# Freeing a PSUM bank with a ScalarE copy, and issuing GpSimd's DMAs from SyncE, in a perceiver layer

## The chip, the cores and the metric

One NeuronCore of a Trainium2 chip runs the whole layer in one launch. The metric is device time in microseconds (us). The engines are TensorE (PE: matmuls; its weight loads are listed apart as PEld), VectorE (DVE), ScalarE (ACT), GpSimd (POOL) and SyncE (SP, which here only issues DMAs). Each engine works through its own instructions in order and waits on semaphores. PSUM, where matmul results arrive, is used here as eight banks of 128 partitions x 512 fp32.

## The reference

Three residual blocks in fp32 on x of 4 x 256 x 256: cross-attention of x on a context of 4 x 4096 x 256, causal linear attention with exponential features, and a gated feed-forward block. Nearly all the time, and all of the change, lies in the first.

```python
def _L0_xattn_ref(query, key, value, Wq, bq, Wk, bk, Wv, bv, Wh, bh):
    Q = query @ Wq.T + bq
    K = key @ Wk.T + bk
    V = value @ Wv.T + bv
    ...
    dot = jnp.einsum('bhsd,bhtd->bhst', Q, K) / np.sqrt(D_HEAD)
    scores = jax.nn.softmax(dot, axis=-1)
    out = jnp.einsum('bhst,bhtd->bhsd', scores, V)
    out = out.reshape(B, T_src, D_MODEL)
    return out @ Wh.T + bh
...
x = x + _L0_xattn_ref(_layernorm(x, axis=-1), ctx_1024, ctx_1024, ...)
x = x + _L0_attn_ref(_layernorm(x, axis=-1), ...)
x = x + _L0_ffn_ref(_layernorm(x, axis=-1), ...)
```

There are 16 heads of 16 dimensions, 256 queries and 4096 context rows for each of 4 batches.

## The kernel before

**Units and steps.** The work is cut into 16 units `u`: a batch and four heads. A unit has 16 steps, one for each 256 context rows, so the main loop runs n = 0 to 256, with w = n modulo 16 the step within the unit. PE, ACT, DVE and SP execute in the order in which the program writes their instructions; the order on POOL is chosen by the framework.

**Softmax in two passes.** The exponentials need each query's maximum first. `maxima(s, heads)` makes it, 19 steps ahead (s = n + 19): for 128 of the queries and 512 context rows, one `pm` tile (a full PSUM bank, L843, two products) for each of four heads, which a `tensor_reduce` on DVE brings down to one column of `mx` (L849). Each step has four `pm` tiles, for heads 0 to 3. At w = 13, `shift(u + 1)` takes the maximum over all columns for the next unit (L857), splits it into a high and a low half `nhl`, and sends it with eight small DMAs as rows into `sh` (L869).

**A step.** `scores` makes for each head a tile `pt` of 256 context rows x 256 queries: a product of ones and `sh` brings the negative maxima in (L893), then four products of keys and queries (L902); `exps` takes the exponential on ACT into `e` (L910). `product` multiplies the previous step's `e` by the values into `pav` (L924), and `add` sums that on DVE into `av` (L938).

**Context items.** Keys and values of later units are made in the same loop. An item is a chunk of 512 context rows for eight heads (two units). Eight key items, then eight value items, are made over two units, each item in two halves, one a step. A half makes a tile `pc` (L183); its `out` brings `pc` to SBUF on ACT: `ku` for keys (L772), `v` for values (L805). For keys, POOL then splits `ku` into two halves `khl` (L752, L753), and SP sends these in four DMAs into the key tiles `kt` (L780). Key items fall into steps w = 8 to 15 of an even unit and w = 0 to 7 of the odd one after it. The item's context comes into one of four slots of `wff` (4 x 1024 of its 4608 columns; later `wff` takes the feed-forward weights). `load_context` issues one such load on SP (L737). Three are issued at the start, and one more when each item is constructed, that is just before its first half.

**Banks.** All PSUM tiles rotate through eight banks in the order in which the program allocates them: a new tile waits until the one allocated eight places before it has been read. In the steps that make maxima and an item's half, that order is pm2, pm3, pt0, pt1, pt2, pt3, pm0, pm1, pc, pav. So pc takes the bank of pm2, pav that of pm3, and in the next step the first six tiles take the banks of pt0 to pt3, pm0, pm1, and the last two `pm` those of pc and pav.

**The end of a unit.** At w = 0, `finish(u - 1)` writes `av` to DRAM (`scr`, L951, and the sums, L953) and, when `scr` has landed, reads it back in another layout (eight DMAs `oT`, L960, and two `dn`, L964), all on POOL; only for the last two units on SP. At w = 8, 9, 10 and 12 of the next unit its reciprocals (L970), its division (L974) and, for odd units, a projection (L987) follow.

**The end of the loop.** In the last steps the second block begins. `plan` lists its pieces by step, 0 being n = 240; the pieces at -4 are the loads of the feed-forward weights into `wff` (L432), which wait for the contexts there to be read. `att0` is a tile for this block's result that takes the place of an earlier one. After n = 236 no maxima are made any more, after n = 235 no items.

Of the kernel before, what the change touches and what calls it, by code (L numbers as in the profile page):

```python
# [12 lines left out]
F32 = mybir.dt.float32  # L13
# [3 lines left out]
ALU = mybir.AluOpType  # L17
AX = mybir.AxisListType
# [3 lines left out]
P = 128  # L22
# [18 lines left out]
def perceiver_layer(  # L41
# [406 lines left out]
    def start_causal():  # L448
# [43 lines left out]
        def call(f, *args):  # L492
            return lambda: f(*args)
# [16 lines left out]
            -15: [call(sq2, 0), v2], -14: [call(sq2, 1)],  # L510
            -13: [call(qk_normed, 0)], -12: [call(qk_normed, 1)],
            -11: [call(qk_turned, 0)], -10: [call(qk_turned, 1)],
            -4: [call(weight_load, n) for n in range(6)],
            -3: [call(features, 0)],
            -1: [steps[0][0]],
            0: [steps[0][1], steps[1][0]],
            1: [call(features, 2)],
# [162 lines left out]
def cross_attention(tc, xr, load_x, load_queries, load_rest, ctxT, wqP, bqu_sb, wkP, bk_sb, wvP, eps,  # L680
# [22 lines left out]
    with ExitStack() as st:  # L703
# [29 lines left out]
        def load_context():  # L733
            for i, (_, p, c) in itertools.islice(loads, 1):
                c0 = i % 4 * KC * CH
                t = wff[:, c0 : c0 + KC * CH].rearrange("p (k c) -> p k c", c=CH)
                nc.sync.dma_start(out=t, in_=ctxT[p // 2, c])  # L737
                contexts.append(t)

        def context(p, c):  # L740
            load_context()
            return contexts.pop(0)

        kts = {}
# [10 lines left out]
        def key(p, c, queues=(nc.sync,) * 4, engine=nc.gpsimd):  # L755

            m, x = p % 2, context(p, c)
            ku = upool.tile([P, CH], F32, tag="ku", name="ku", bufs=2)
            khl = upool.tile([P, 2, CH], F32R, tag="khl", name="khl", bufs=2)
            made = []  # L760

            def half(part, pk):
                made.append(pk)
                cs = slice(part * (CH // 2), (part + 1) * (CH // 2))
                for k in range(KC):
                    product4(
                        pk, wk_sb[:, k, m * P : (m + 1) * P], x[:, k, cs], start=k == 0, stop=k == KC - 1
                    )

            def out(part):  # L770
                cs = slice(part * (CH // 2), (part + 1) * (CH // 2))
                nc.scalar.activation(ku[:, cs], made.pop(), AF.Identity, bias=bk_sb[:, m : m + 1])  # L772
                if part == 0:
                    return
                halved((khl[:, 0], khl[:, 1]), ku, engine)
                for u in (2 * p, 2 * p + 1):
                    kts[u, c] = key_tile(u % 3, c, F32R)
                for h in range(4):
                    half, side = divmod(h, 2)
                    queues[h].dma_start(  # L780
                        out=kts[2 * p + half, c][side::2].bitcast(F32),
                        in_=khl[64 * half : 64 * half + 64, side].bitcast(F32),
                    )

            return half, out

        def value(p, c):

            m, x = p % 2, context(p, c)
            made = []  # L790

            def half(part, pv):
                pv = pv.rearrange("p (i t) -> p i t", t=P)
                made.append(pv)
                for i in range(2):
                    t0 = (2 * part + i) * P
                    for k in range(KC):
                        product4(
                            pv[:, i, :], x[:, k, t0 : t0 + P], wv_sb[:, k, m * P : (m + 1) * P],
                            start=k == 0, stop=k == KC - 1,  # L800
                        )

            def out(part):
                to = vs[:, c, 2 * part : 2 * part + 2, : 8 * (HD + 1)]
                nc.scalar.copy(  # L805
                    to.rearrange("p t (h d) -> p t h d", d=HD + 1)[:, :, :, :HD],
                    made.pop().rearrange("p t (h d) -> p t h d", d=HD),
                )

            return half, out  # L810

        def whole(item):
            half, out = item
            for part in range(2):
                half(part, bank([P, CH // 2], "pc"))
                out(part)
# [14 lines left out]
        def maxima(s, heads):  # L831

            u, w = divmod(s, NS)
            c, i = divmod(w, 2)
            if u not in mxs:
                mxs[u] = small.tile([P, 2, 4, NCH], F32, tag="mx", name="mx")
            mx, qa, kt = mxs[u], qas[u], kts[u, c]
            pms = [bank([P, CH], "pm") for _ in heads]

            def products(turn):  # L840
                for j, pm in zip(heads, pms):
                    rows = slice(32 * j, 32 * j + 32)
                    nc.tensor.matmul(  # L843
                        pm, lhsT=qa[rows, turn, i::2], rhs=kt[rows, :], start=turn == 0, stop=turn == 1
                    )

            def reduce():
                for j, pm in zip(heads, pms):
                    nc.vector.tensor_reduce(mx[:, i, j, c : c + 1], pm, AX.X, ALU.max)  # L849

            return products, reduce

        def shift(u):

            sh = shs[u] = small.tile([P, T], F32R, tag="sh", name="sh")
            neg = small.tile([P, 4, 2], F32, tag="neg", name="neg")
            nc.vector.tensor_reduce(neg.rearrange("p j i -> p i j"), mxs.pop(u), AX.X, ALU.max, negate=True)  # L857
            if u == 0:
                by_head = neg.rearrange("p j i -> p i j")
                hi, lo = neg0[:, :, :, 0], neg0[:, :, :, 1]  # L860
                nc.vector.tensor_copy(hi.bitcast(F32R), by_head)
                nc.vector.tensor_tensor(lo, by_head, hi, ALU.subtract)
            else:
                nhl = small.tile([P, 4, 2, 2], F32R, tag="nhl", name="nhl")
                halved((nhl[:, :, 0], nhl[:, :, 1]), neg, nc.vector)
                for j in range(4):
                    for side in range(2):
                        row = 32 * j + side
                        nc.gpsimd.dma_start(  # L869
                            out=sh[row : row + 1, :].rearrange("o (p i) -> o p i", i=2).bitcast(F32),  # L870
                            in_=nhl[:, j, side].bitcast(F32),
                        )

# [10 lines left out]
        def scores(n, heads):  # L884

            u, w = divmod(n, NS)
            kt, qa, sh = kts[u, w // 2], qas[u], shs[u]
            pts = [bank([P, 2, T], "pt") for _ in heads]

            def shifts():  # L890
                for j, pt in zip(heads, pts):
# [48 lines left out]
        def finish(u):  # L940
# [5 lines left out]

            b, q = divmod(u, NQ)
            av = avs.pop(u)
            queue = nc.sync if u >= NU - 2 else nc.gpsimd
            scr = dram.tile([P, T], F32, tag="scr", name="scr")  # L950
            queue.dma_start(out=scr, in_=av)  # L951
            sums = dram.tile([T // 16, 4, 16], F32, tag="sums", name="sums")
# [73 lines left out]
        with tc.manual_schedule(engines={ET.PE, ET.Activation, ET.DVE, ET.SP}):  # L1026
# [35 lines left out]
            qs[0][2](0, nc.vector)  # L1062
            normal[1][0]()
            unit_queries(0)
            whole(key(0, 0, (nc.sync, nc.scalar) * 2, nc.vector))
            unit_queries(1)
            for piece in normal[1][1:]:
# [47 lines left out]
            def all_maxima(g, between=None):  # L1115

                groups = [maxima(g, heads) for heads in ((0, 1), (2, 3))]
                for turn in range(2):
                    for products, _ in groups:
                        products(turn)  # L1120
                for _, reduce in groups:
# [18 lines left out]
            later = {}  # L1140
            plan = {}
            masks(wide.tile([P, 3, P], F32, tag="mask", name="mask"))
            att0 = wide.tile([P, KC, D], F32, tag="wk", name="att0")
            place["att"] = lambda b: att0
            tags = itertools.cycle(("ku", "khl"))
            place["at"] = lambda: upool.tile([P, 3, P], F32, tag=next(tags), name="at", bufs=2)
            place["sq"] = lambda: upool.tile([P, CH], F32, tag="ku", name="sq", bufs=2)
# [5 lines left out]
            for n in range(NU * NS + 1):  # L1153
# [3 lines left out]
                if n < NU * NS:  # L1157
                    s = n + NS + LEAD
                    if s < NU * NS:
                        most0, reduce0 = maxima(s, (2, 3))  # L1160
                        (shift0, first0, exps0), (shift1, first1, exps1) = [scores(n, h) for h in ((0, 1), (2, 3))]
                        most1, reduce1 = maxima(s, (0, 1))
                        most0(0)
                        shift0()
                        most0(1)
# [8 lines left out]
                        first1(1, 0)  # L1174
                        most1(1)
                        first1(1, 1)
                        reduce0()
                        exps0()
                        exps1()
                        reduce1()  # L1180
                    else:
                        firsts = [scores(n, heads) for heads in ((0, 1), (2, 3))]
                        for shifts, products, exps in firsts:
# [109 lines left out]
```

## Time and profile before

| what | us |
|---|---|
| median of 3 runs (1108.57, 1109.46, 1111.49) | 1109.46 |
| the profiled execution | 1106.57 |
| its span, first to last instruction | 1104.5 |
| PE busy | 1054.9 (96%) |
| DVE busy | 899.1 (81%) |
| ACT busy | 692.5 (63%) |
| POOL busy | 358.8 (32%) |
| granted PE clock, mean | 0.992 |
| first step of the main loop begins | 73 |
| step 208 begins (causal pieces between) | 805 |
| step 237 begins (no more maxima) | 924 |
| last value product of the loop ends | 986 |

A quiet step of the main loop, between the starts of its first shift products, lasts 3.39 to 3.40 us. In such a step, by windows of one step, DVE is busy for 2.90 us, ACT for 2.33. Matmul ends in the profile are modelled and matmuls overlap, so a PE that shows as busy may still stand. In a group's row the columns are: line, engine, operation, output and inputs with shapes, count, then busy time in us and mean ns of one, then the engine's idle time just before these and what ended most of it. A timeline row starts with the start and the length in us.

### The profile page before, as it was taken

The page shows a single profiled execution, that of the slowest core. Times are in us where ns is not written, and L with a number is a line of the kernel's source. Part 1 is how long each engine was busy: PE and PEld are TensorE (multiplying, and loading weights), DVE is VectorE, ACT ScalarE, POOL GpSimd, SP SyncE. Part 2 cuts the span into 40 slices and gives each one's busy share as a digit, 9 for nine tenths or more (in the row PEclk, how much of TensorE's full clock was granted, in tenths as well). Part 3 has the DMA queues.
Part 4 walks back from the last instruction along what each step waited for, and adds up shares of the span by engine and source line. Part 5 has one row for each costly group of instructions (what it writes and reads, how often), then busy time and mean ns, then how long its engine had stood idle before and what let it go on. Part 6 is the DMA issues. An engine that isn't in the chain of part 4 may idle for free.

```text
span 1104.5 us, 44721 instructions
## 1 busy us (share of the span) xinstructions
PE 1054.9 (96%) x19032; PEld 730.7 (66%) x19032; DVE 899.1 (81%) x1754; ACT 692.5 (63%) x1439; POOL 358.8 (32%) x571
## 2 busy tenths in 40 slices
PE   6999989999999999999999999999999999999998
PEld 4467657766766677657766776577666666666777
DVE  4998878888888888878888888799898898576753
ACT  3346766666666666666666666666664457875442
POOL 3421442244224422441245224523352324123110
PEclk8999999999999999999999999999999999999999
DMA  8664562356335633553346434643355111000000
GB/s 258 165 200 121 151 171 86 89 150 163 99 94 136 169 106 96 135 158 114 100 110 177 114 101 106 162 126 96 102 148 141 46 45 52 12 10 8 6 11 20
DMA packets 64798, 120.20 MB, mean 109 GB/s; under 512 B 21248, under 2 KB 29368, under 8 KB 64600
## 3 DMA queue, kind: packets, MB, share of 16 engines
q1 hardware_dynamic: 54312, 112.61, 36.5%
q0 software_dynamic: 9568, 3.96, 2.2%
q8 instruction: 150, 2.46, 0.9%
q10 hardware_dynamic: 720, 0.79, 0.2%
q14 instruction: 48, 0.39, 0.1%
HBM read 76.13 MB, written 3.21 MB: 72 GB/s over the span
## 4 chain that ended last, share of the span: by engine, by line
PE 66%; DVE 21%; POOL 4%; DMA 4%; issue 2%; ACT 1%; SPq 0%; ACTq 0%; DVEq 0%; POOLq 0%
PE pc L183 20%; PE pav L924 18%; DVE mx L849 16%; PE pm L843 10%; POOL oT L960 3%; PE pt L902 3%; DMA scr<-av 2%; DMA kt<-khl 2%; PE pg L587 2%; PE pd L603 2%; PE pu L587 2%; DVE av L938 2%; PE pa L339 2%; PE pqk L183 1%; PE pt L893 1%
## 5 line engine op out<-in xcount | busy, mean ns | idle before, releaser
L910 ACT ACTIVATE e<-pt 128x512 f32<-128x512 f32 x1024 | 528.8, 604 | 296.8 <-PE pt L902 292.5
L849 DVE TENSOR_REDUCE mx<-pm 128x1 f32<-128x512 f32 x1024 | 632.9, 681 | 50.3 <-PE pm L843 48.9
L843 PE MATMUL pm<-kt,qa 32*128 32x512 f32 x2048 | 352.8, 426 | 17.4 <-DMA kt<-khl 15.0
L902 PE MATMUL pt<-qa,kt 32*128 32x256 f32 x4096 | 281.2, 278 | 0.0
L902 PEld LDWEIGHTS pt<-qa,kt 32*128 32x128 f32 x4096 | 270.1, 184 | 7.3
L924 PE MATMUL pav<-e,v 128*32 128x256 f32 x4096 | 270.7, 381 | 0.1
L843 PEld LDWEIGHTS pm<-kt,qa 32*128 32x128 f32 x2048 | 161.5, 191 | 127.9 <-ACT e L910 70.0
L893 PE MATMUL pt<-sh,ones 2*128 2x512 f32 x1024 | 226.4, 449 | 0.5 <-ACT e L910 0.4
L924 PEld LDWEIGHTS pav<-e,v 128*32 128x32 f32 x4096 | 129.1, 110 | 73.6 <-issue 5.3
L183 PE MATMUL pc<-wff,wk_sb 128*32 128x256 f32 x2048 | 140.0, 396 | 10.5 <-DVE mx L849 4.8
L938 DVE TENSOR_TENSOR av<-pav,av 128x256 f32<-128x256 f32 x240 | 101.6, 423 | 58.3 <-PE pav L924 57.7
L183 PE MATMUL pc<-wv_sb,wff 128*32 128x128 f32 x4096 | 137.3, 276 | 11.3 <-DVE mx L849 5.4
L183 PEld LDWEIGHTS pc<-wv_sb,wff 128*32 128x32 f32 x4096 | 104.3, 109 | 36.8 <-DVE mx L849 36.0
L752 POOL CAST khl<-ku 128x512 fp32r<-128x512 f32 x63 | 39.3, 624 | 268.1 <-ACT ku L772 247.5
L893 PEld LDWEIGHTS pt<-sh,ones 2*128 2x128 f32 x1024 | 93.7, 182 | 11.8 <-ACT e L910 4.1
L183 PEld LDWEIGHTS pc<-wff,wk_sb 128*32 128x32 f32 x2048 | 56.0, 112 | 62.1 <-DVE mx L849 33.2
L869 POOL DMA_DIRECT2D sh<-nhl x120 | 64.7, 555 | 69.0 <-PE pt L902 42.5
L753 POOL TENSOR_TENSOR khl<-ku,khl 128x512 fp32r<-128x512 f32 x63 | 80.6, 1279 | 5.1
L960 POOL DMA_DIRECT2D oT<-scr x112 | 66.5, 627 | 27.7 <-DMA scr<-av 22.6
L772 ACT ACTIVATE ku<-pc,bk_sb 128x256 f32<-128x256 f32 x128 | 63.1, 494 | 14.4 <-PE pc L183 11.4
L805 ACT COPY v<-pc 128x256 f32<-128x256 f32 x128 | 51.7, 404 | 10.1 <-PE pc L183 10.0
L977 POOL TENSOR_TENSOR oT<-oT,bvT 128x64 f32<-128x64 f32 x32 | 8.7, 292 | 82.3 <-DVE oT L974 80.7
(150 smaller groups left out, 703.0 us busy)
## 6 DMA issues: line engine op xcount, KB each, us to landing
wff<-in_ctxT_dram SPq DMA_DIRECT2D x128, 512.0 KB
kt<-khl SPq DMA_DIRECT2D x254, 128.0 KB
qa<-qhl SPq DMA_DIRECT2D x64, 64.0 KB
sh<-nhl POOLq DMA_DIRECT2D x120, 1.0 KB, 3.2
scr<-av POOLq DMA_DIRECT2D x14, 128.0 KB, 2.3
oT<-scr POOLq DMA_DIRECT2D x112, 8.0 KB, 2.2
xr<-in_x_dram SPq DMA_DIRECT2D x4, 256.0 KB
out_dram<-o SPq DMA_DIRECT2D x8, 128.0 KB
```

The lines of the kernel that those rows point to most:

```text
L183: nc.tensor.matmul(out[js], lhsT=lhsT[:, js], rhs=rhs, **flags)
L753: engine.tensor_tensor(lo, x, hi.bitcast(F32), ALU.subtract)
L772: nc.scalar.activation(ku[:, cs], made.pop(), AF.Identity, bias=bk_sb[:, m : m + 1])
L843: nc.tensor.matmul(pm, lhsT=qa[rows, turn, i::2], rhs=kt[rows, :], start=turn == 0, stop=turn == 1)
L849: nc.vector.tensor_reduce(mx[:, i, j, c : c + 1], pm, AX.X, ALU.max)
L869: nc.gpsimd.dma_start(out=sh[row : row + 1, :].rearrange("o (p i) -> o p i", i=2).bitcast(F32), in_=nhl[:, j, side].bitcast(F32),)
L893: nc.tensor.matmul(pt, lhsT=ones[rows, :], rhs=sh[rows, :].unsqueeze(1).to_broadcast([2, 2, T]), start=True, stop=False,)
L902: nc.tensor.matmul(pt[:, i, :], lhsT=kt[rows, k0 : k0 + P], rhs=qa[rows, turn], start=False, stop=i == 1 and turn == 1,)
L910: nc.scalar.activation(e, pt, AF.Exp, scale=0.25)
L924: nc.tensor.matmul(pav[32 * h : 32 * h + 32, :], lhsT=v[:, t % KT, c0 : c0 + 32], rhs=es[n, h][:, i, :], start=i == 0, stop=i == 1,)
L938: nc.vector.tensor_tensor(avs[u], pav, avs[u], ALU.add)
L960: queue.dma_start(out=oT[:, k, q % 2, j], in_=scr[32 * j : 32 * j + HD, k * P : (k + 1) * P].rearrange("e (r a) -> r e a", a=16),)
```

## The change

The first `pm` tile of a step is now head 3's, and its bank is emptied by a ScalarE copy to SBUF; VectorE takes that head's maxima from the copy, after the step's other three. The eight banks are taken in another order: pm3, pm2, pt0, pt1, pt2, pm0, pt3, pm1, pc, pav. So pc takes the bank of pm3, pav that of pm2, and the next step's tiles take, in that order, the banks of pt0, pt1, pt2, pm0, pt3, pm1, pc and pav. The order of the products on PE stays. Two buffers hold the copies in turn: the last 512 columns of `wff` and a tile of `wide`; for that, `att0` is allocated only at its first use and the weights' loads come one step later.

The eight DMAs of `shift` and all DMAs of `finish` are issued by SP instead of POOL. A context's load is no longer issued when an item is constructed, but after the products of its second half, into the slot that these have just read; four loads are issued at the start instead of three.

```diff
-            -4: [call(weight_load, n) for n in range(6)],
-            -3: [call(features, 0)],
+            -3: [*(call(weight_load, n) for n in range(6)), call(features, 0)],
...
         def context(p, c):
-            load_context()
             return contexts.pop(0)
...
+                if part == 1:
+                    load_context()
...
+        copies = []
+
+        def maxima(s, heads, banks=None):
...
-            pms = [bank([P, CH], "pm") for _ in heads]
+            pms = banks or [bank([P, CH], "pm") for _ in heads]
...
-            def reduce():
-                for j, pm in zip(heads, pms):
-                    nc.vector.tensor_reduce(mx[:, i, j, c : c + 1], pm, AX.X, ALU.max)
-
-            return products, reduce
+            def reduce(only=heads, of=dict(zip(heads, pms))):
+                for j in only:
+                    nc.vector.tensor_reduce(mx[:, i, j, c : c + 1], of[j], AX.X, ALU.max)
+
+            def copied(j):
+                to = copies[s % 2]
+                nc.scalar.copy(to, pms[heads.index(j)])
+                return {j: to}
+
+            return products, reduce, copied
...
-                        nc.gpsimd.dma_start(
+                        nc.sync.dma_start(
                             out=sh[row : row + 1, :].rearrange("o (p i) -> o p i", i=2).bitcast(F32),
...
-            queue = nc.sync if u >= NU - 2 else nc.gpsimd
+            queue = nc.sync
...
             unit_queries(0)
+            load_context()
             whole(key(0, 0, (nc.sync, nc.scalar) * 2, nc.vector))
...
-            att0 = wide.tile([P, KC, D], F32, tag="wk", name="att0")
-            place["att"] = lambda b: att0
+            copies.extend((wff[:, 4 * KC * CH :], wide.tile([P, CH], F32, tag="wk", name="copy")))
+            atts = []
+
+            def att0(b):
+                if not atts:
+                    atts.append(wide.tile([P, KC, D], F32, tag="wk", name="att0"))
+                return atts[0]
+
+            place["att"] = att0
...
-                        most0, reduce0 = maxima(s, (2, 3))
-                        (shift0, first0, exps0), (shift1, first1, exps1) = [scores(n, h) for h in ((0, 1), (2, 3))]
-                        most1, reduce1 = maxima(s, (0, 1))
+                        pm3, pm2 = [bank([P, CH], "pm") for _ in range(2)]
+                        pt0, pt1, pt2 = [bank([P, 2, T], "pt") for _ in range(3)]
+                        pm0, pt3, pm1 = bank([P, CH], "pm"), bank([P, 2, T], "pt"), bank([P, CH], "pm")
+                        most0, reduce0, copied = maxima(s, (3, 2), (pm3, pm2))
+                        shift0, first0, exps0 = scores(n, (0, 1), (pt0, pt1))
+                        shift1, first1, exps1 = scores(n, (2, 3), (pt2, pt3))
+                        most1, reduce1, _ = maxima(s, (0, 1), (pm0, pm1))
...
-                        reduce0()
+                        copy = copied(3)
+                        reduce0((2,))
                         exps0()
                         exps1()
                         reduce1()
+                        reduce0((3,), copy)
```

More of the change, by code (lines that the diff above doesn't have):

```diff
@@ L801, in half @@
                         )
+                if part == 1:
+                    load_context()
             def out(part):
@@ L829, in unit_queries @@
                     )
-        def maxima(s, heads):
+        copies = []
+        def maxima(s, heads, banks=None):
             u, w = divmod(s, NS)
@@ L882, in shift, with scores @@
             return turn
-        def scores(n, heads):
+        def scores(n, heads, banks=None):
             u, w = divmod(n, NS)
             kt, qa, sh = kts[u, w // 2], qas[u], shs[u]
-            pts = [bank([P, 2, T], "pt") for _ in heads]
+            pts = banks or [bank([P, 2, T], "pt") for _ in heads]
             def shifts():
@@ L1064, in cross_attention @@
             unit_queries(0)
+            load_context()
             whole(key(0, 0, (nc.sync, nc.scalar) * 2, nc.vector))
@@ L1118, in all_maxima @@
                 for turn in range(2):
-                    for products, _ in groups:
+                    for products, *_ in groups:
                         products(turn)
-                for _, reduce in groups:
+                for _, reduce, _ in groups:
                     if between is not None:
```

## The prediction

> **What bounds the kernel now.** I first read the shares of the chain that ended last, then the costliest groups, then the same chain inside a quiet stretch of the main loop, then a timeline around each doubtful point.
>
> ```profile
> PE 66%; DVE 21%; POOL 4%; DMA 4%; issue 2%; ACT 1%; SPq 0%; ACTq 0%; DVEq 0%; POOLq 0%
> L849 DVE TENSOR_REDUCE mx<-pm 128x1 f32<-128x512 f32 x1024 | 632.9, 681 | 50.3 <-PE pm L843 48.9
> ...
> 304.95 0.69 DVE mx L849
> 305.64 0.04 issue
> 305.68 1.08 PE pc L183 x32
> 306.76 0.86 PE pav L924 x16
> 307.63 0.43 PE pm L843
> 308.06 0.12 PE pt L902
> 308.18 0.16 PE pm L843 x2
> 308.34 0.69 DVE mx L849
> ```
>
> The page has TensorE 96% busy, yet VectorE holds 21% of the chain, and nearly all of that is one maximum per step. The pieces of the stretch (start, length, what) show one step of 3.39 us as a loop: the first maximum, 0.69 us, then 0.04 us, then the context products pc, the value products pav, the next step's pm, and again the first maximum. The reason is the PSUM rotation. Before, a step takes its eight banks in the order pm2, pm3, pt0, pt1, pt2, pt3, pm0, pm1, pc, pav, so pc gets the bank of pm2, which VectorE must have read.
>
> Does TensorE really stand there? The next rows (start, length, engine, line) compare the turn from score products to another kind of product, first where pc waits, then late, where the step has no maxima.
>
> ```profile
> 305.33 0.28 PE L902 MATMUL pt<-qa,kt 32*128 32x256 f32 x2
> 305.68 1.08 PE L183 MATMUL pc<-wv_sb,wff 128*32 128x128 f32 x32
> ...
> 953.67 0.64 PE L902 MATMUL pt<-qa,kt 32*128 32x256 f32 x16
> 954.24 1.07 PE L924 MATMUL pav<-e,v 128*32 128x256 f32 x16
> ```
>
> In the first pair pc begins 0.07 us after the modelled end of the last score product. In the second the next kind begins 0.07 us before it (953.67 + 0.64 = 954.31). Over all such turns the median from the last score start is 0.34 us with pc, 0.20 without a wait. So at most 0.14 us a step can be had here.
>
> **The change part by part.** *Copy of the first tile.* pm3 now comes first, pc takes its bank, and the bank is free when ScalarE has copied it. No 128x512 copy from PSUM stands in the main loop; these rows are nearest:
>
> ```profile
> L294 ACT COPY qkT<-tr_qk 128x512 f32<-128x512 f32 x2 | 1.1, 588 | 1.6 <-PE tr_qk L291 1.6
> L231 ACT COPY zT<-tr 128x512 f32<-128x512 f32 x1 | 0.6, 585 | 0.3 <-PE tr L230 0.3
> ...
> 305.25 2.06 ACT L910 ACTIVATE e<-pt 128x512 f32<-128x512 f32 x4 [1.07 <-PE pt L902]
> 307.17 0.41 ACT L805 COPY v<-pc 128x256 f32<-128x256 f32 x1
> ```
>
> I take 0.59 us: 0.09 under the 0.68 of the reduction. The step then lasts about 3.30 us and TensorE keeps a gap of 0.25, above its 0.20. Steps that make pc: 232. Leaving a dozen that stall elsewhere, 220 x 0.09 = 20 us gained. Bounds: the gap closes fully, 220 x 0.14 = 31 gained; or the copy costs as the slowest ScalarE row of this size, the features' ACTIVATE at 0.727, 220 x 0.046 = 10 lost. I choose by the copy rows, the same operation and shape.
>
> Behind the copy on ScalarE wait the four exponentials, and for their banks the next step's products. ScalarE idles 1.07 us ahead of the exponentials. The copy starts with the old reduction (304.94); the first exponential follows one pitch later (2.06 for four is 0.48 to 0.52 each), near 305.46 instead of 305.25. The last bank comes free 0.2 us later, near 307.5, and its new user, the second pair of shift products, starts 0.58 us into the next step (304.74 - 304.16), so after 308. Priced at 0; without that cover, up to 0.2 a step. The pc bank, read out last, now goes to pt3, in the same pair; its slack is about 0.2.
>
> VectorE keeps four reductions, one from SBUF. That price is not shown for this shape; the 128x512 reduction of squares from SBUF is 0.677, so no change.
>
> [...]
>
> *VectorE's other work.* Where it is late, its first maximum is late and so is pc: steps 9 and 10 of a unit last 3.49 (a reciprocal of 0.54 each), step 13 about 0.25 over (the shift's 0.21 + 0.17 + 0.17). With pc off VectorE this goes: 13 units x (0.20 + 0.27) = 6, of which I take 5, since pav still waits for the reduction of pm2, with 0.9 us of pc ahead of it. From step 185 on, causal pieces load VectorE too: 1.5, between 0 and 5.
>
> *GpSimd's DMAs on SP.* Moved: 120 issues for the shifts (8 a unit, 0.55 each) and 14 x 12 for the outputs (scr, sums, 8 oT, 2 dn). SP's own rows for the output chain, 938.99 to 947.05, make 8.1 us with the wait for scr; GpSimd needed 9.2 to 10.1. What this chain holds up:
>
> ```profile
> 478.00 0.68 POOL L964 DMA_DIRECT2D dn<-sums  x1
> 478.58 0.72 POOL L752 CAST khl<-ku 128x512 fp32r<-128x512 f32 x1
> 479.33 3.11 SPq L780 DMA_DIRECT2D kt<-khl  x4
> 483.09 0.50 PE L843 MATMUL pm<-kt,qa 32*128 32x512 f32 x2 [1.78 <-DMA kt<-khl]
> 484.58 1.79 PE L183 MATMUL pc<-wff,wk_sb 128*32 128x256 f32 x16
> ```
>
> GpSimd issues until 478.68, only then splits the keys; the key DMAs land late and TensorE waits 1.78 us. Seven odd units do this, 10.4 us in all (15.0 less 4.6 at the start). Three times the granted clock then fell to half for 3.4 us (pc 1.79 instead of 1.07), 1.5 us more each.
>
> [...]
>
> After: GpSimd splits early, but SP, in order, has the output chain, then the context load (now issued inside the key's own step), then the key DMAs. With av ready at 468.5: chain done 476.6, load issued, second key DMA near 478.5. A lone key DMA landed 2.26 us after its issue (480.69), 0.6 of it its own 128 KB at the 208 GB/s of the stretch 596 to 599; so 1.6 fixed, 2.5 for the load's 512 KB, 1.3 for two key DMAs: landing near 482.0 instead of 482.95, while the step starts 0.4 us sooner. Gain 0.5 us where the wait was 1.8 or more (three units), nothing where it was 1.0, and one of the three slow stretches avoided: 3 x 0.5 + 1.5 = 3 us taken. Bounds: all 15 gained; or wait and slow clock in all seven (7 x 4.6 = 32), 17 lost. The shifts' 8 x 0.58 = 4.6 us end with some 2 us of slack before the unit (landing near 575.5, needed 578).
>
> *Start.* Behind the first key's products a second 512 KB load precedes the key DMAs (issued 16.18, landed 20.6): 2 us lost, between 0 and 3. Other loads keep six steps of lead: 0.
>
> *Weights one step later*, behind SP's last shifts, near 930 instead of 897, landing near 943; their first product is at 988.8: 0. Without that cover, the 11 us of transfer (2.3 MB at 208 GB/s).
>
> **Sum:** -20 - 5 - 1.5 - 3 + 2 = -27.5 us on the profiled execution of 1106.57 (span 1104.5): 1079. That execution lies 2.9 under the median of the runs shown, 1109.46; the forecast median is 1082.
>
> **The rivals.** *SP gives it back* (1102). The key DMAs land behind chain and load, TensorE waits 3 us and cools in seven units: +17 in place of -3, net -7.5. For it: one ordered queue. Against it: SP's scr took 1.8 us, GpSimd's 4.0 there.
>
> [...]
>
> *ScalarE becomes the bound* (1118, slower). Its work by single durations is 0.588 + 4 x 0.604 + 0.404 = 3.41 in value steps and 3.50 in key steps (0.494), over 3.39 by 0.02 and 0.11. It decides as soon as ScalarE can't overlap successive instructions: 220 x 0.06 = 13 lost, 5 of VectorE regained, about +8.5 with the start. Against it: four exponentials take 2.06, and L805 starts 0.14 before they end.
>
> *The turn isn't a wait* (1107): TensorE needs 0.34 to turn to pc whatever frees the bank, so only small terms stay, -2.5. Against: 0.20 at 954.
>
> *More than forecast* (1057): the whole gap, all stalls and VectorE's delays go: -31 - 6 - 15 - 2 + 1.5 = -52.
>
> **Numbers.** Forecast 0.52 (own range 1074 to 1092); SP 0.13; ScalarE 0.16; no wait 0.12; more 0.07. A difference of 0.3%, 3.3 us, is about what can be told. Faster: 0.52 + 0.11 of SP's + 0.07 + 0.04 of the no-wait case = 0.74. Same: 0.01 + 0.07 = 0.08. Slower: 0.16 + 0.01 + 0.01 = 0.18. The range 1062 to 1111 leaves out ScalarE's case and 0.03 of the best: 0.19.
>
> **What would show it.** The quiet step at 3.30 us; in its chain an ACT copy of 0.59 where VectorE's 0.69 stood; steps 9, 10 and 13 no longer longer; the odd units' key wait under 1 us with at most one slow-clock stretch. A step above 3.36 with ScalarE busy over 95% would make the forecast wrong, as would key waits of 3 us.

## The result and the profile after

The changed kernel takes **1123.06 us** (median of 4 runs, 1121.51 to 1126.61) against 1109.01 for the kernel before (4 runs, 1108.22 to 1111.49): a ratio of 1.0127, with an interval of 1.0098 to 1.0157. It is slower by about 14 us, where 27 us less were forecast. Its profiled execution took 1122.44 us, with a span of 1120.7 and a mean granted clock of 0.977.

These lines are the granted clock by slices, the shares of the chain that ended last and four groups, from the page of the kernel after.

```profile
PEclk8999989998999999999998999899999998999999
...
PE 83%; DVE 6%; DMA 6%; ACT 2%; POOL 1%; issue 1%; SPq 1%; ACTq 0%; POOLq 0%
...
L855 DVE TENSOR_REDUCE mx<-pm 128x1 f32<-128x512 f32 x787 | 506.1, 684 | 83.8 <-PE pm L849 79.5
...
L849 PE MATMUL pm<-kt,qa 32*128 32x512 f32 x2048 | 362.7, 432 | 37.7 <-DMA kt<-khl 33.7
...
L859 ACT COPY copy<-pm 128x512 f32<-128x512 f32 x119 | 69.8, 587 | 74.9 <-PE pm L849 74.9
...
L855 DVE TENSOR_REDUCE mx<-copy 128x1 f32<-128x512 f32 x119 | 80.4, 675 | 0.0
```

The reader should see two things in them. VectorE's share of the chain fell from 21% to 6% and TensorE's rose from 66% to 83%: the wait for VectorE that the copy was to take away is gone, and a shorter one for the copy stands in its place (below). And the group of the maxima's products now stands 33.7 us for key DMAs, with dips in the clock where there were few. What was won step by step was lost in a few places.

The quiet step's chain after (start, length, what), once round the loop:

```profile
422.01 1.04 PE pc L183 x32
423.06 0.86 PE pav L935 x16
423.92 0.43 PE pm L849 x2
...
425.18 0.12 PE pt L913 x2
425.30 1.03 PE pc L183 x32
```

No other engine is left in it; the step lasts 3.29 us. The timeline of ScalarE and of pc's weight load beside it (start, length, engine, line):

```profile
424.62 0.59 ACT L859 COPY wff<-pm 128x512 f32<-128x512 f32 x1 [0.46 <-PE pm L849]
425.10 2.07 ACT L921 ACTIVATE e<-pt 128x512 f32<-128x512 f32 x4
425.25 0.81 PEld L183 LDWEIGHTS pc<-wv_sb,wff 128*32 128x32 f32 x32 [0.16 <-ACT wff L859]
```

The copy ends at 425.21. The chain names the step's last score products instead, which end later by the profile's model (425.30). Yet pc begins a median 0.053 us after the copy's end, as it began 0.056 us after the reduction's end before: the copy still lets it go. The wait is shorter, not gone. Its sums, by what ended it (total, times, longest), before and then after:

```profile
PEld pc L183 <- DVE mx L849: 69.2, 226, 0.8
```

```profile
PEld pc L183 <- ACT copy L859: 17.2, 102, 0.4
...
PEld pc L183 <- ACT wff L859: 15.2, 91, 0.2
```

ScalarE still stands 0.46 us ahead of the copy.

**Where the time went.** The steps' own starts (the first shift product of each), read from the two profiled executions, split the 16.2 us by which the span grew:

| stretch | before | after | difference |
|---|---|---|---|
| up to step 0 | 73.35 | 76.72 | +3.4 |
| steps 0 to 236 | 850.95 | 854.46 | +3.5 |
| of it: first eight steps of the odd units 1 to 13, over eight quiet steps | 17.7 | 46.6 | +28.9 |
| of it: the rest | 833.3 | 807.9 | -25.4 |
| steps 237 to 254 | 57.18 | 66.50 | +9.3 |
| of it: step 240 | 4.50 | 13.82 | +9.3 |
| the rest | 123.05 | 123.05 | 0 |

The third row is called the odd units' excess below (3.3 us of it, in unit 13, are causal pieces and not a stall, as a version without stalls will show). A wait stands behind each of the two big losses.

**The keys of the odd units.** SP's issues in unit 7 of the kernel after, and the product that waits (start, length, what):

```profile
468.50 3.11 SPq L780 DMA_DIRECT2D kt<-khl  x4
471.71 0.53 SPq L962 DMA_DIRECT2D scr<-av  x1
472.29 0.60 SPq L964 DMA_DIRECT2D sums<-av  x1
475.51 2.50 SPq L971 DMA_DIRECT2D oT<-scr  x4
478.13 0.57 SPq L975 DMA_DIRECT2D dn<-sums  x1
478.75 2.75 SPq L971 DMA_DIRECT2D oT<-scr  x4
481.55 0.57 SPq L975 DMA_DIRECT2D dn<-sums  x1
482.23 0.40 SPq L736 DMA_DIRECT2D wff<-in_ctxT_dram  x1
482.73 2.48 SPq L780 DMA_DIRECT2D kt<-khl  x4
...
475.06 0.61 POOL L750 CAST khl<-ku 128x512 fp32r<-128x512 f32 x1 [5.23 <-ACT ku L772]
...
488.01 0.51 PE L849 MATMUL pm<-kt,qa 32*128 32x512 f32 x2 [3.51 <-DMA kt<-khl]
```

GpSimd is free now: it starts to split these keys at 475.06, where before it could not until 478.58. But its result is ready at 477.05 and SP sends it only from 482.73, behind the ten issues that read the outputs back and a context load. The chain holds SP from 471.71 to 482.12, and in 2.6 us of it (472.89 to 475.51) SP issues nothing at all: it stands for scr to land. TensorE stands 3.51 us, where it stood 1.78. The same wait comes in all seven odd units, 3.3 to 4.7 us each, and after it the clock is low. The windows' row (us, busy time of PE, PEld, DVE, ACT, POOL, then granted clock, DMA share, GB/s) for the wait and what follows:

```profile
484.00:492.00 8.00, 4.49 (x64) 2.63 (x59) 3.51 (x6) 3.75 (x8) 0.00 (x0) 0.81 0.81 251
```

Between 85 and 930 us the granted clock was 0.5 for 37.5 us in this execution, 10.2 us in that of before.

**Step 240.** The timeline of the kernel after, GpSimd, SP and TensorE:

```profile
932.30 5.75 SPq L880 DMA_DIRECT2D sh<-nhl  x8
938.14 1.01 SPq L432 DMA_DIRECT2D wff<-in_w_gate_dram  x2
...
941.49 0.83 POOL L436 TENSOR_SCALAR wff<-wff 128x768 f32<-128x768 int32 x1 [4.06 <-DMA wff<-in_w_gate_dram]
...
948.00 0.83 POOL L436 TENSOR_SCALAR wff<-wff 128x768 f32<-128x768 int32 x1 [1.25 <-DMA wff<-in_w_down_dram]
948.78 0.77 POOL L351 TENSOR_SCALAR_AFFINE_SELECT at<-at 128x256 f32<-128x256 f32 x2
...
949.25 1.86 PE L365 MATMUL po<-at,va 128*32 128x256 f32 x16 [7.18 <-POOL at L351]
```

The weights are loaded one step later and behind the eight DMAs of the last shift, so they land from 941 on. GpSimd scales each as it lands, in the order of its instructions, and the causal mask of the second block (L351) is queued behind the last scaling. TensorE stands 7.18 us for that mask. Before, the scalings were done by 925.

### The profile page after: what moved, and what is told of

Read it like the earlier page. It is cut to its first block, busy times and chain, and to the rows that moved or that the text cites. A ratio compares the mean times of both kernels' runs of the same rounds, so it can differ in the third digit from the quotient of the medians.

```text
span 1120.7 us, 45110 instructions
## 1 busy us (share of the span) xinstructions
PE 1065.7 (95%) x19032; PEld 741.4 (66%) x19032; DVE 909.7 (81%) x1754; ACT 809.5 (72%) x1676; POOL 195.2 (17%) x283
## 3 DMA queue, kind: packets, MB, share of 16 engines
q8 instruction: 150, 2.46, 0.9%
## 4 chain that ended last, share of the span: by engine, by line
PE 83%; DVE 6%; DMA 6%; ACT 2%; POOL 1%; issue 1%; SPq 1%; ACTq 0%; POOLq 0%
PE pc L183 21%; PE pav L935 18%; PE pm L849 16%; PE pt L913 10%; DVE mx L855 5%; DMA kt<-khl 4%; PE pt L904 4%; PE pg L586 2%; PE pd L602 2%; PE pu L586 2%; PE pa L339 2%; PE pqk L183 1%; PE po L365 1%; ACT e L921 1%; PE pf L313 1%
## 5 line engine op out<-in xcount | busy, mean ns | idle before, releaser
L855 DVE TENSOR_REDUCE mx<-pm 128x1 f32<-128x512 f32 x787 | 506.1, 684 | 83.8 <-PE pm L849 79.5
L849 PE MATMUL pm<-kt,qa 32*128 32x512 f32 x2048 | 362.7, 432 | 37.7 <-DMA kt<-khl 33.7
L913 PE MATMUL pt<-qa,kt 32*128 32x256 f32 x4096 | 288.1, 281 | 0.0
L913 PEld LDWEIGHTS pt<-qa,kt 32*128 32x128 f32 x4096 | 274.9, 187 | 6.6
L849 PEld LDWEIGHTS pm<-kt,qa 32*128 32x128 f32 x2048 | 166.2, 194 | 151.7 <-ACT e L921 77.5
L183 PE MATMUL pc<-wff,wk_sb 128*32 128x256 f32 x2048 | 143.9, 404 | 0.0
L859 ACT COPY wff<-pm 128x512 f32<-128x512 f32 x118 | 69.2, 587 | 96.2 <-PE pm L849 96.2
L859 ACT COPY copy<-pm 128x512 f32<-128x512 f32 x119 | 69.8, 587 | 74.9 <-PE pm L849 74.9
L855 DVE TENSOR_REDUCE mx<-copy 128x1 f32<-128x512 f32 x119 | 80.4, 675 | 0.0
L855 DVE TENSOR_REDUCE mx<-wff 128x1 f32<-128x512 f32 x118 | 79.7, 675 | 0.0
```

The costliest lines, as they stand in the source:

```text
L183: nc.tensor.matmul(out[js], lhsT=lhsT[:, js], rhs=rhs, **flags)
L849: nc.tensor.matmul(pm, lhsT=qa[rows, turn, i::2], rhs=kt[rows, :], start=turn == 0, stop=turn == 1)
L855: nc.vector.tensor_reduce(mx[:, i, j, c : c + 1], of[j], AX.X, ALU.max)
L859: nc.scalar.copy(to, pms[heads.index(j)])
L913: nc.tensor.matmul(pt[:, i, :], lhsT=kt[rows, k0 : k0 + P], rhs=qa[rows, turn], start=False, stop=i == 1 and turn == 1,)
```

## The experiments

Two questions had to be told apart: is the copy worth what was forecast, and which of the moves on SP and GpSimd takes it back? Ten kernels; the ratio is to the kernel before, run beside them. All compute the whole output. "Excess" is the odd units' excess, "key waits" the sum of TensorE's waits for key DMAs after 80 us (10.5 in the kernel before), "low" the length of the stretches at a granted clock of 0.5 that begin between 85 and 930 us (10.2 of e4's lie at step 240), each from the one profiled execution.

| run | median us (runs) | ratio [interval] | excess | key waits | low | step 240 |
|---|---|---|---|---|---|---|
| after | 1123.06 (4) | 1.0127 [1.0098, 1.0157] | 46.6 | 27.3 | 37.5 | 13.82 |
| e1_copy_alone | 1089.78 (4) | 0.9819 [0.9779, 0.9859] | 24.2 | 14.2 | 13.7 | 4.50 |
| e2_weights_back | 1117.87 (8) | 1.0065 [1.0044, 1.0085] | 47.8 | 29.9 | 41.0 | 4.50 |
| e3_loads_back | 1107.73 (10) | 0.9972 [0.9949, 0.9995] | 34.7 | 19.3 | 27.3 | 14.09 |
| e4_finish_pool | 1105.59 (10) | 0.9954 [0.9934, 0.9975] | 28.8 | 16.8 | 27.3 | 14.04 |
| e5_split_after | 1071.97 (4) | 0.9651 [0.9622, 0.9681] | 3.2 | 0 | 0 | 4.50 |
| e6_order_only | 1111.84 (10) | 1.0011 [0.9990, 1.0031] | 23.4 | 13.2 | 17.1 | 4.50 |
| e7_copy_old_order | 1091.08 (4) | 0.9816 [0.9777, 0.9854] | 25.1 | 15.5 | 17.1 | 4.21 |
| e8_split_copy | 1070.53 (4) | 0.9641 [0.9608, 0.9675] | 3.3 | 0 | 0 | 4.50 |
| e9_split_pool | 1078.58 (4) | 0.9710 [0.9672, 0.9747] | 12.7 | 5.8 | 3.4 | 4.50 |
| e10_split_before | 1099.31 (4) | 0.9899 [0.9865, 0.9932] | 8.1 | 5.3 | 0 | 4.50 |

**e1_copy_alone: the copy without the moves.** The kernel after, with the DMAs of shift and finish, the context loads and the weights where they were before:

```diff
-            -3: [*(call(weight_load, n) for n in range(6)), call(features, 0)],
+            -4: [call(weight_load, n) for n in range(6)],
+            -3: [call(features, 0)],
...
-                        nc.sync.dma_start(
+                        nc.gpsimd.dma_start(
...
-            queue = nc.sync
+            queue = nc.sync if u >= NU - 2 else nc.gpsimd
...
         def context(p, c):
+            load_context()
             return contexts.pop(0)
...
```

> The copy, its bank order and its buffers as in the changed kernel; all DMAs, context loads and weight loads as before the change. Theory A (the copy is worth about 28 us, and what SP was given costs it all back): quiet steps of 3.28 to 3.30 us, odd units' key waits near those before the change (1 to 2.5 us each, a little more because steps are shorter), no wait for the weights, first step at 73 us, and 1083 to 1089 us in all. Theory B (the copy stands ahead of ku on ScalarE and shorter steps bring the keys' deadline forward, so the copy itself makes the key waits): waits of 3 to 5 us in the odd units remain, and the time is 1100 us or more.

Measured: 1089.78 us, ratio 0.9819; the quiet step 3.284. So the copy is worth about 20 us of 1109 and the moves cost some 34 (1.0127 - 0.9819 = 0.031). The time lies just above theory A's 1083 to 1089 and far below B's 1100. The odd units' keys were no better for it: they come by the old way, GpSimd's chain first. That their excess is above that of the kernel before (24.2 and 17.7) need not be the shorter steps' doing, since e6, with the old steps, has 23.4; each is one execution. The waits in the two kernels, e1 first (total, times, longest), then after:

```profile
PE pm L847 <- DMA kt<-khl: 14.2, 7, 3.0
```

```profile
PE pm L849 <- DMA kt<-khl: 33.7, 9, 6.5
```

The row of the kernel after counts the start's wait of 6.5 us too, which in e1 ends with another DMA and stands in another row; without it some 27 us in eight waits are left.

**e2, e3, e4: one move undone at a time.** Each is the kernel after with one of the hunks above taken back: the weights' step (e2), the context loads (e3), the output chains' queue (e4).

```diff
-            -3: [*(call(weight_load, n) for n in range(6)), call(features, 0)],
+            -4: [call(weight_load, n) for n in range(6)],
+            -3: [call(features, 0)],
```

> The changed kernel with the six weight loads issued one step earlier again, as before the change, ahead of the last shift's DMAs on SP. Theory A (the loads, issued at 938 us behind the shift, keep GpSimd waiting, and GpSimd's masks of the second block stand behind the weights' scaling): step 240 goes from 13.8 us back to about 4.5, and the time from 1123 to about 1114 us. Theory B (step 240 is long because the last unit's shift rows arrive late from SP): step 240 stays above 10 us and the time at 1121 to 1124 us.

```diff
         def context(p, c):
+            load_context()
             return contexts.pop(0)
...
-                if part == 1:
-                    load_context()
...
             unit_queries(0)
-            load_context()
             whole(key(0, 0, (nc.sync, nc.scalar) * 2, nc.vector))
```

> The changed kernel with the context loads issued at an item's construction again, three at the start. Theory A1 (the 512 KB load that SP now issues just ahead of the key DMAs delays their landing by about 2.3 us): the odd units' waits fall from 3.3-4.8 to about 1-2.5 us, the slow-clock stretches to at most four, the first step comes at 73 us instead of 76.7; 1123 becomes 1095 to 1104 us. Theory A2 (the output chain alone, in SP's order, makes the waits): the waits fall by less than 0.7 us each, the time to 1113-1119 us, 3 us of that from the start.

```diff
-            queue = nc.sync
+            queue = nc.sync if u >= NU - 2 else nc.gpsimd
```

> The changed kernel with the output chains (scr, sums, oT, dn) on GpSimd again, except those of the last two units; shifts and loads stay as changed. Theory A1 (the load ahead of the keys is the larger part): key DMAs go out when GpSimd has split the keys behind the chain, load no longer just ahead of them since SP issued it earlier, waits of 1 to 2.5 us, 1097 to 1106 us. Theory A2 (the chain on SP is the cause): the same waits, so this run alone does not tell A1 from A2; with the run that puts the loads back it does: if both undo most of the waits, it is the pair that costs. If instead waits stay above 3 us here, neither holds and the keys are late on ScalarE.

Measured: e2 brings step 240 from 13.82 back to 4.50 us and leaves the odd units as they were (excess 47.8); its ratio is 0.006 below that of the kernel after, some 7 us, where theory A gave 9. GpSimd's mask is then no longer behind the scalings but waits for ScalarE, as this row of e2 shows:

```profile
945.95 0.78 POOL L351 TENSOR_SCALAR_AFFINE_SELECT at<-at 128x256 f32<-128x256 f32 x2 [3.69 <-ACT at L350]
```

e3 and e4 leave step 240 at 14.0 and each takes part of the odd units' excess: 11.9 us of it with the loads back, 17.8 with the chain back on GpSimd, where both together (e1, which also takes back shift's DMAs and the weights) take 22.4. So neither alone is the cause. Counted from e1, by the medians and without the 9.3 us of step 240, the chain on SP adds some 9 us (e3: 1107.73), the late loads some 6 (e4: 1105.59), and both together 28 (e2: 1117.87, which has step 240 as before): behind one another on one queue they cost more than their sum. Shift's DMAs are on SP in all three. Either, taken away, leaves keys that are late: e3, with the chain still on SP, has waits of 1.9 to 3.5 us, more than theory A1 gave, and a time between its two theories.

**e5_split_after: keep every DMA on SP, cut the chain.** If what hurts is that SP stands in one piece for scr and ten issues just ahead of keys, the moves themselves should be harmless once the chain is cut. e5 is e2 with the reading back moved out of `finish`: scr and the sums at w = 0 as before, the first five DMAs (`back(0)`) at w = 2, the other five at w = 4.

```diff
-            for k in range(KC):
+            def back(k):
...
-            return [lambda: one_over(0), lambda: one_over(1), divide] + ([project] if q % 2 == 1 else [])
+            backs = [lambda: back(0), lambda: back(1)]
+            return backs, [lambda: one_over(0), lambda: one_over(1), divide] + ([project] if q % 2 == 1 else [])
...
-                    left = finish(u - 1)
+                    backs, left = finish(u - 1)
+                    if u == NU:
+                        for piece in backs:
+                            piece()
                     if u < NU:
+                        later[n + 2], later[n + 4] = backs
```

> The changed kernel with the weight loads one step earlier, and with each output chain cut in three on SP: scr and sums at step 0 of a unit as now, the first four oT and a dn at step 2, the others at step 4. All other DMAs and the context loads stay on SP as changed. Theory A (the key DMAs are late because they stand in SP's order behind one uncut chain that waits for scr): the odd units' key waits fall from 3.3-4.7 us to under 1 us, nearly no slow clock, and the time is 1072 to 1085 us, below the copy alone. Theory C (SP and its DMA queue simply have too much to do, the load ahead of the keys most of all): waits of 2 to 4 us stay, somewhere in the odd units, and the time is 1100 to 1116 us.

Measured: 1071.97 us, ratio 0.9651, against 1.0065 for e2: some 46 us by this edit alone. No odd unit waits for keys any more, and the clock stays up. SP's timeline in unit 7 of e5, and the windows' row of the same stretch:

```profile
454.24 0.53 SPq L963 DMA_DIRECT2D scr<-av  x1
454.82 0.60 SPq L965 DMA_DIRECT2D sums<-av  x1
455.52 0.39 SPq L737 DMA_DIRECT2D wff<-in_ctxT_dram  x1
457.35 3.12 SPq L781 DMA_DIRECT2D kt<-khl  x4
460.57 2.54 SPq L972 DMA_DIRECT2D oT<-scr  x4
463.15 0.57 SPq L976 DMA_DIRECT2D dn<-sums  x1
464.13 0.33 SPq L737 DMA_DIRECT2D wff<-in_ctxT_dram  x1
464.58 2.65 SPq L781 DMA_DIRECT2D kt<-khl  x4
467.28 2.67 SPq L972 DMA_DIRECT2D oT<-scr  x4
```

```profile
449.00:466.00 17.00, 17.00 (x316) 10.90 (x308) 15.54 (x27) 15.19 (x33) 5.69 (x6) 1.00 0.71 196
```

Keys now go out between the pieces of the chain: 457.35 is 3.1 us after scr, where the kernel after sent the corresponding ones 11 us after it (482.73 - 471.71). scr lands while keys are being sent, and no time is spent on it. TensorE is busy for all 17 us at full clock. The loads just ahead of the keys are still there (455.52, 464.13) and hurt nobody. The edit takes away two things at once, SP's wait for scr and the ten issues in one piece; which of them weighs more was not tried by itself.

**e6 and e7: which half of the edit works, bank order or copy?** e6 is e1 without the copy, with the reduction of head 3 from PSUM again; e7 is e1 with the copy but the old order of banks, so that head 2's tile, which comes first there, is the one that is copied.

```diff
-                        copy = copied(3)
-                        reduce0((2,))
+                        reduce0()
...
-                        reduce0((3,), copy)
```

> All DMAs as before the change, the new order of the banks, but no copy: VectorE reduces all four tiles, head 3 first. The reduction of head 3 isn't taken from a copy. Theory A (pc waits for the 0.68 us reduction, whichever head's): quiet steps of 3.39 us, steps 9, 10 and 13 longer again, 1108 to 1113 us. Rival (the order of the banks is what helps): quiet steps of 3.28 to 3.32 us and a time under 1095 us.

```diff
-                        pm3, pm2 = [bank([P, CH], "pm") for _ in range(2)]
-                        pt0, pt1, pt2 = [bank([P, 2, T], "pt") for _ in range(3)]
-                        pm0, pt3, pm1 = bank([P, CH], "pm"), bank([P, 2, T], "pt"), bank([P, CH], "pm")
...
+                        most0, reduce0, copied = maxima(s, (2, 3))
...
-                        copy = copied(3)
-                        reduce0((2,))
+                        copy = copied(2)
+                        reduce0((3,))
...
-                        reduce0((3,), copy)
+                        reduce0((2,), copy)
```

> All DMAs as before the change, the copy of the step's first tile (head 2 here), but the banks taken in the order of before. Theory A (the copy alone carries the gain, the order only lets tiles that ScalarE reads come later): quiet steps of 3.28 to 3.31 us and 1086 to 1094 us. Rival (with the copy ahead of the exponentials the old order makes the next step's tiles wait for VectorE's later reductions or for the last exponential): quiet steps of 3.33 us or more and 1100 us or more.

Measured: e6 1.0011, its interval around 1, quiet step 3.393; e7 0.9816, quiet step 3.284, the same as e1. The copy alone does it, and the new order of banks brings nothing that can be measured.

**e8, e9, e10: which queue, and what the cut is worth by itself.** e8 is e1 with the chain on SP and cut as in e5 (shift's DMAs stay on GpSimd, loads at construction). e9 is e1 with the same cut and the chain on GpSimd. e10 is the kernel before with that cut on GpSimd.

```diff
-            queue = nc.sync if u >= NU - 2 else nc.gpsimd
+            queue = nc.sync
```

> The copy with the shifts on GpSimd and context loads and weight loads as before the change; only the output chains on SP, cut in three over steps 0, 2 and 4. Theory A: GpSimd splits the keys at once, SP sends them between the pieces of the chain, key waits under 1 us, 1070 to 1080 us, the fastest of all. Theory C: waits of 1.5 to 3 us stay and the time is 1085 to 1100 us.

> The copy, with every DMA and load where it was before the change (output chains on GpSimd), but each chain cut in three over steps 0, 2 and 4 as in the fastest kernels so far. Theory D (what stands in the keys' way is one uncut chain on whichever engine carries it, since the keys pass through GpSimd first and SP after): the odd units' key waits go as on SP, at most 0.5 us each, 1070 to 1078 us. Theory E (GpSimd is the wrong place even in pieces, since each piece of some 3 us still delays a key split by as much): waits of 0.5 to 2 us stay and the time is 1079 to 1090 us.

> The kernel before the change, with nothing but its output chains on GpSimd cut in three. Under D: quiet steps stay at 3.39, the key waits (10.5 us in seven units) and the slow clock behind some of them go, 1093 to 1098 us, a ratio to the kernel before of 0.985 to 0.990; the copy's gain and this one add up to that of the run beside it. Under E: 1098 to 1108 us.

Measured: e8 1070.53 us, ratio 0.9641, the fastest; e5's interval covers the same. So shift's DMAs and the later loads on SP are worth nothing that shows, and with the chain cut they cost nothing either. The chain's shares and the clock of e8's page:

```profile
PEclk8999999999999999999999999999999999999999
...
PE 90%; DVE 7%; DMA 1%; ACT 1%; issue 0%; ACTq 0%; SPq 0%; DVEq 0%
```

e9, at 0.9710, keeps about three fifths of the cut's gain: key waits of 1.1 to 2.1 us remain. Its time lies on the border between what the two theories gave it: cutting is what counts, but GpSimd is the worse place for the pieces, since the waits that remain are those that theory E gave. Its timeline in unit 7:

```profile
459.49 2.36 POOL L969 DMA_DIRECT2D oT<-scr  x4 [3.22 <-DMA scr<-av]
461.80 0.63 POOL L973 DMA_DIRECT2D dn<-sums  x1
462.38 1.23 POOL L969 DMA_DIRECT2D oT<-scr  x2
463.53 0.69 POOL L752 CAST khl<-ku 128x512 fp32r<-128x512 f32 x1
464.08 0.67 POOL L969 DMA_DIRECT2D oT<-scr  x1
...
468.51 0.51 PE L847 MATMUL pm<-kt,qa 32*128 32x512 f32 x2 [1.16 <-DMA kt<-khl]
```

GpSimd stands 3.22 us for scr ahead of the first piece, and the key's split (463.53) comes between the DMAs of the second. The engine that must split the keys is the one that issues. e10, at 0.9899, takes 1% from the kernel before. Theory D had its ratio right (0.985 to 0.990) and the waits wrong: they were to go, and 5.3 of 10.5 us stay, four waits of 1.0 to 1.9. What went entirely is the slow clock, and its 1099.31 us lie in theory E's range. 0.9899 x 0.9819 (e1) is 0.9720, within e9's interval, so copy and cut add up.

The rows show the wait itself: in the kernel after, SP stands 2.6 us between sums and oT (472.89 to 475.51) with the keys behind it; in e5 the dependent issues, written later, go out 0.1 us after the keys' (457.35 + 3.12 = 460.47, then oT at 460.57), and no key waits.

## Why the prediction was wrong

**The copy: right, and a little under-sized.** Forecast were a copy of 0.59 us (measured 0.587), a step of 3.30 (3.285) and 0.09 us a step; it is 0.111, because the reduction that pc waited for, the step's first, took a median 0.691 us against 0.586 for the copy, and not the mean of all reductions, 0.681, that the working used. The median gap ahead of pc falls from 0.344 to 0.236 us, not to the 0.20 of a turn without a wait. Steps 9, 10 and 13, 3.49, 3.49 and 3.65 us before, take 3.28 now: that term was right as well. The causal pieces' 1.5 us did not come: 16 steps from 208 take 70.78 us before and, without the odd unit's extra stall (8.5 - 3.5), 68.8 after, no more than the other steps gain; from 224 on nothing is gained at all (58.00 and 58.19). Steps 0 and 1 got 1.4 us longer; the cause is open. In all, -25.4 us of -26.5; that the sum comes so near is partly luck, the larger gain a step covering what did not come.

**"GpSimd's DMAs on SP ... 3 us taken": this step failed.** In place of 3 gained, the odd units lost 28.9 us more than before. The working had the right chain and the right objects in it, and set three of its terms by rows from another place, two of them from a quieter one:
- SP's scr "took 1.8 us", from the tail. Here the oT issue comes 3.8 us after scr's, 2.0 more. In the seven odd units of the kernel after it is 3.0 to 4.9 us; in the even ones, where no keys are made early in the unit, it is 1.7 to 1.8 in all but one (3.8). The tail's row and unit 7's differ in what the DMA engines carry meanwhile, by the windows (the last two numbers are the DMA share and GB/s), first before in the tail, then after in the loop:

```profile
939.00:940.80 1.80, 1.80 (x44) 1.23 (x40) 0.60 (x2) 1.40 (x3) 0.00 (x0) 1.00 0.24 75
```

```profile
471.70:475.50 3.80, 3.80 (x80) 2.70 (x76) 3.09 (x6) 3.04 (x7) 0.43 (x1) 1.00 0.56 161
```

- The load and the keys behind the chain took 5.9 us from its end to the first product (482.12 to 488.01), forecast 5.4 (476.6 to 482.0). The ten issues took 6.6, where the tail's took 6.3.
- Together 2.8 us in unit 7. Over all seven units the key waits are 27.3 us, 10.5 before, and 9.0 were forecast (10.5 less 3 x 0.5): 18 too many. The low clock does the rest: 6.8 us of it were to remain, 37.5 came, and at about 1.5 us for each 3.4 of low clock this is 13.5 more. The two make the 32 us from -3 to +29.

So "landing near 482.0 instead of 482.95" was an answer inside its own error: a gain of half a microsecond in a chain of 13, with a term from a stretch that moved 75 GB/s where unit 7 moved 161. The upper bound, 17 lost, allowed 4.6 us a unit, 3 of wait and one slow stretch; the excess is 6.2 (46.6 less 3.3, by seven), since the waits are 3.3 to 4.7 and in four of the units the clock was low for 6.83 us.

**"Their first product is at 988.8: 0" failed too.** The weights indeed are not missed by their own product. The 9.3 us are lost by an instruction that has nothing to do with them and stands behind their scaling on GpSimd. The working named GpSimd's queue for the keys and not for the weights; e2 shows that the step's return alone brings the 9.3 back.

**The start** was forecast at +2 and is +3.4. This is not settled: with the loads as before, step 0 begins between 73.4 and 76.4 us in the profiled executions of before, e1, e6, e7, e8 and e10, and the clock's low stretches fall elsewhere in each.

**The rivals.** *SP gives it back* had the mechanism and a chance of 0.13; its price of 17 was 12 too small. 1102 + 12 + 9.3 for step 240 is 1123. *ScalarE becomes the bound* did not come: it idles a median 0.47 us before the copy, and its first exponential starts 0.48 after the copy does. *The turn isn't a wait* is ruled out by e1's 3.284 and the chain above. *More than forecast* needed a second change that this one doesn't make, the cut of e5 and e8; even these stay 13 us above its 1057.

## What to carry to other kernels

Before DMAs are moved to another queue, list everything that stands behind each of them there, on the issuing engine and on whatever engine handles what the DMA brings, and price each in the busiest stretch it will meet, not in a quiet one (the 1.8 us taken for scr from the tail were 3.8 in unit 7). A chain with a wait inside it (write, wait until it has landed, read back) should be cut at the wait, the parts written some steps apart: in three parts, two steps apart, this was worth 46 us with the chain and the late loads on SP and 11 in the kernel before, and with it the moves of the other DMAs made no difference. And a wait that is removed step by step is best tried without the edits that ride along: the copy alone gave 1.8%, with its companions it was 1.3% slower.

## What the runs showed of the hardware

**The granted clock dropped after some short waits and not after others.** In the kernel before it was at 0.5 for 3.4 us after a wait of 1.78 us (481.3 to 483.1) and after those of 2.46 and 2.27 (ending at 146.4 and 708.8); it stayed at full speed after those of 1.37, 0.92, 0.92 and 0.73. In e1 it fell after waits of 1.76 and 1.92, in e9 after one of 1.46. A wait of 2.25 in e1 (146.2 to 148.4) left it at full speed. Two windows of e1, behind the wait of 2.25 and behind that of 1.92 (granted clock third from the end):

```profile
148.50:152.00 3.50, 3.50 (x64) 2.43 (x68) 2.74 (x5) 2.82 (x6) 0.00 (x0) 1.00 0.95 247
256.50:260.00 3.50, 3.50 (x48) 2.31 (x52) 2.38 (x4) 2.56 (x5) 0.00 (x0) 0.59 0.96 242
```

Low stretches within the loop lasted 3.41 or 6.83 us (one in e2 10.24), and their starts lay whole multiples apart of 3.413 us, the length of each in the kernel before (there, 484.8 - 146.9 = 337.9 is 99.0 of them). On that grid the 1.76 and 1.92 of e1 fall into one period each, and the 2.25 is cut into 1.7 and 0.5. But the place in the period does not decide alone: in e4 a wait of 1.73 (259.2 to 260.9) also lies within one period and the clock stayed at full speed, and in e2 even one of 2.65 (488.7 to 491.3) did not lower it. What decides is open: no run moved a wait of one length against the grid.

**A reduction from SBUF took nearly what one from PSUM took**: 675 beside 684 ns for 128x512, both in the kernel after. **scr, a 128 KB write to DRAM issued by SP, was followed by its reading back 1.8 us later in the tail (before) and 3.8 in the loop (after, unit 7)**, with 75 and 161 GB/s moved meanwhile; that the traffic is the cause was not tried by itself.
